# Layer 0 attention: scores on 32x64 pieces of the array, reciprocals of row sums on transposed blocks, five groups of key tiles added up

## The chip, the core and the metric

The kernel runs on one core of one Trainium2 chip. A core has five engines that work side by side and wait for each other by semaphores: TensorE (PE in the profile; its weight loads are a row of their own, PEld), VectorE (DVE), ScalarE (ACT), GpSimd (POOL) and SyncE (SP), which here issues DMAs. The metric is the device time of one execution, in microseconds (us). Matmuls write to PSUM, which here is used as six banks for three score tiles and two banks for two accumulators; everything else lies in SBUF.

## The reference

Four layers, each of the form x = x + f(groupnorm(x)), on x of 2 images, 128 channels, 64x64 pixels. Only layer 0 is touched by the change. Its f, cut to what matters:

```python
xn = biasfree_ln(x, ln1_w)
qkv = conv1x1(xn, w_qkv)
qkv = depthwise_conv3x3(qkv, w_dw)
q1, k1, v, q2, k2 = split(qkv, 5)                 # 4 heads of 32 channels, 4096 tokens
q1, q2, k1, k2 = l2norm over the tokens
attn1 = softmax(einsum('bhnc,bhmc->bhnm', q1, k1) * temperature)   # 4096 x 4096 per head
out1 = einsum('bhnm,bhmc->bhnc', attn1, v)
attn2 = softmax(einsum('bhnc,bhnd->bhcd', q2, k2) * temperature)   # 32 x 32 per head
out2 = einsum('bhnc,bhcd->bhnd', v, attn2)
out = conv1x1(out1 + out2, w_po)
out = conv1x1(biasfree_ln(out, ln2_w), w_proj) + b_proj
```

Layer 1 is a sum of small convolutions and correlations, layer 2 a quaternion convolution by FFT, layer 3 a softmax attention with 8 heads over the same 4096 tokens.

## The kernel before, in words

All is float32. For each image, layer 0 first runs its convolutions, then the large attention (`attention`, line 1750), then `finish` (line 1803), which multiplies by the output weights and is woven into the convolutions of the next image.

The attention goes over 8 blocks of 512 queries (`qb`), and in each over 32 tiles of 128 keys (`kt`); a pair of the two is a step here. One step of `_attn_four` (line 1333) does this for all four heads:

- four score matmuls (line 1341), one per head `j`. The stationary operand is 32 channels by 128 keys of `k1`, the moving one 32 channels by 512 queries of `q1`. Head `j` lies in partitions 32j to 32j+31, so that the four use four different row groups of the array. The result, keys by queries, goes to a PSUM tile of two heads (`ps_s`, two tiles a step out of three buffers).
- two exps on ScalarE (line 1350), one for each PSUM tile, into a `weights` tile of 128 x 4 x 512 in SBUF (four buffers).
- for the step before, `multiply` (line 1774): four value matmuls (line 1757), each 128 keys by 32 channels of `vt`, which write 32 partitions each of one accumulator, `ac[0]`. They use four column groups of the array and add up over the 32 key tiles of the block.

The softmax needs the sums over the keys as well. VectorE adds up the weights of `SUMMED` = 8 key tiles into one `sums` tile (line 1792, seven additions a group, since the first tile of a group is only remembered), and `sums` (line 1759) multiplies each finished group by a matrix of ones of 32 columns into the second accumulator, `ac[1]`: four matmuls, again of line 1757, for each of four groups in a block. It is called at the fourth step of the group after. As ones have 32 equal columns, each row sum comes out 32 times, once for each channel of its head.

With the last group of a block, `sums` also divides: ScalarE copies the accumulator (line 1770) into a tile with the tag `g`, which has one buffer and is used for the normalised input of the next image as well (line 1484); VectorE takes reciprocals of its 128 x 512 elements (line 1771) and multiplies the values by them into `q1` (line 1772), whose queries of this block are no longer needed. The values have been copied to `used` by ScalarE at the last key tile (line 1782).

Other work is woven in: every four steps of the attention one piece of a side list goes in (`_weave`). The list is the small channel attention of both images, and for image 0 the normalisation of image 1 (`normalize`, line 1473), for image 1 some statistics.

Within the convolutions and `finish` the order of each engine's instructions is that of the program. Within the attention it isn't held: there the planner of the tile framework orders the instructions by the program's order and by its own estimate of when they are ready. Each engine then works through its own queue in that order, and waits where an operand isn't there.

Of the kernel before, what the change touches and what calls it, by code (L numbers as in the profile page):

```python
# [10 lines left out]
F32 = mybir.dt.float32  # L11
# [7 lines left out]
CH = 512  # L19
NCH = S // CH  # L20
ROWS = CH // W
NQT = S // 128
# [92 lines left out]
def _weave(main, side, every):  # L115

    for n, _ in enumerate(main):
        if n % every == every - 1:
            next(side, None)
    for _ in side:  # L120
        pass
# [1163 lines left out]


LIMIT = 60.0
SUMMED = 8
F32R = mybir.dt.float32r
ENGINES = (  # L1290
    mybir.EngineType.PE,
# [41 lines left out]
def _attn_four(nc, p_pool, ps_pool, q, k, multiply):  # L1333

    waiting = []
    for qb in range(NCH):
        for kt in range(NQT):
            ps = [ps_pool.tile([128, 2, CH], F32, tag="sp", name="ps_s") for _ in range(2)]
            for j in range(4):
                rows = slice(32 * j, 32 * j + 32)  # L1340
                nc.tensor.matmul(  # L1341
                    ps[j // 2][:, j % 2, :],
                    k[rows, kt * 128 : (kt + 1) * 128],
                    q[rows, qb * CH : (qb + 1) * CH],
                    start=True,
                    stop=True,
                )
            w = p_pool.tile([128, 4, CH], F32, tag="weights", name="weights")
            for p in range(2):
                nc.scalar.activation(w[:, 2 * p : 2 * p + 2, :], ps[p], AF.Exp)  # L1350
            waiting.append((qb, kt, w))
            if len(waiting) > 1:
                multiply(*waiting.pop(0))
            yield
    for x in waiting:
        multiply(*x)
    yield
# [49 lines left out]
def _layer0(ctx, tc, X, a, cst, worst, there, dram):  # L1407
    nc = tc.nc
    one = ctx.enter_context(tc.tile_pool(name="f0_one", bufs=1))
    small = ctx.enter_context(tc.tile_pool(name="f0_small", bufs=2))  # L1410
    cp = ctx.enter_context(tc.tile_pool(name="f0_ch", bufs=2))
# [6 lines left out]
    def acc(n):  # L1418
        return accp.tile([128, CH], F32, tag=f"acc{n}", name=f"ps_acc{n}")
# [14 lines left out]
    q1 = one.tile([128, S], F32, name="q1")  # L1434
# [7 lines left out]
    ones = one.tile([128, 32], F32, name="ones")  # L1442
# [307 lines left out]
    def attention(pool, side):  # L1750
        ac = [None, None]
        parts, pending, used = [None], [], {}

        def four(n, lhs, w, first, last):
            for j in range(4):
                rows = slice(32 * j, 32 * j + 32)
                nc.tensor.matmul(ac[n][rows, :], lhs(rows), w[:, j, :], start=first, stop=last)  # L1757

        def sums():

            while pending:
                qb, n, w = pending.pop(0)
                if n == 0:
                    ac[1] = acc(1)
                four(1, lambda rows: ones, w, n == 0, n == NQT // SUMMED - 1)
                if n == NQT // SUMMED - 1:

                    cols = slice(qb * CH, (qb + 1) * CH)
                    rec = cp.tile([128, CH], F32, tag="g", name="rec", bufs=1)
                    nc.scalar.copy(rec, ac[1])  # L1770
                    nc.vector.reciprocal(rec, rec)
                    nc.vector.tensor_mul(q1[:, cols], used.pop(qb), rec)

        def multiply(qb, kt, w):


            if kt == 0:
                ac[0] = acc(0)
            four(0, lambda rows: vt[:, kt, rows], w, kt == 0, kt == NQT - 1)
            if kt == NQT - 1:  # L1780
                used[qb] = pool.tile([128, CH], F32, tag="used", name="used", bufs=2)
                nc.scalar.copy(used[qb], ac[0])  # L1782
            i = kt % SUMMED
            if i == 3:
                sums()
            if i == 0:
                parts[0] = w
            else:
                t = parts[0]
                if i == 1:  # L1790
                    parts[0] = pool.tile([128, 4, CH], F32, tag="sums", name="sums", bufs=2)
                nc.vector.tensor_add(  # L1792
                    parts[0].rearrange("p j c -> p (j c)"),
                    t.rearrange("p j c -> p (j c)"),
                    w.rearrange("p j c -> p (j c)"),
                )
            if i == SUMMED - 1:
                pending.append((qb, kt // SUMMED, parts[0]))

        _weave(_attn_four(nc, pool, spp, q1, k1, multiply), side, 4)  # L1800
        sums()

    def finish(b, w2):
# [78 lines left out]
    for b in range(B):  # L1882
        w2 = small.tile([128, 128], F32, tag="w2", name="w2")
        with tc.tile_pool(name="f0_conv", bufs=1) as pool, _in_order(tc):
            ss2, own = convolutions(pool, b, before)
        if b == 0:

            with _after(tc):
                rows_of_weights = _weights_by_rows(nc, dram, a)
        side = [channel_attention(ss2, own, w2)]  # L1890
        if b + 1 < B:
            side.append(normalize(b + 1))
        if b:
            side.append(
                _stats_steps(
                    nc,
                    small,
                    lambda: sp()[:, 0, :],
                    X[:, b - 1, :],
                    cst,  # L1900
                    mhalf,
                    there[:, b - 1],
                )
            )
        with tc.tile_pool(name="f0_p", bufs=4) as pool:
            attention(pool, chain(*side))
        before = finish(b, w2)
# [434 lines left out]
```

## Time and profile before

| what | time |
|---|---|
| median of three runs | 4225.66 us (4211.73 to 4226.44) |
| span of the profiled execution, which has no other time of its own | 4221.3 us |
| attention of image 0 | about 191 to 815 us of the span |
| attention of image 1 | about 1016 to 1609 us |
| one block of 512 queries, undisturbed | 72.71 us |
| blocks 0, 1, 2 of image 0 | 83.9, 93.3, 75.7 us |
| blocks 0 and 2 of image 1 | 77.8, 75.6 us |
| busy in an undisturbed block (665.5 to 738.2 us) | PE 72.4, DVE 67.6, ACT 63.0 us |
| busy over the whole span | PE 4050.3, DVE 2186.7, ACT 3342.7 us |

How to read it: "busy" of TensorE is not its bound, because its records overlap[...]. The time of one of TensorE's stages is read from the start of one group to the start of the next. Each float32 matmul leaves two records of a load and two of a matmul, called its first and second pass below. Idle time is given with what ended it.

### The profile page before, as it was taken

To read this page: it belongs to the slowest core of one execution; us is meant where nothing else is said; L and a number is where in the kernel's file an instruction comes from. 1 tells how busy PE (TensorE), PEld (TensorE's weight loads), DVE (VectorE), ACT (ScalarE), POOL (GpSimd) and SP (SyncE) were. 2 spreads that over 40 slices of the span, in tenths; PEclk is the share of its full clock that TensorE was granted. 3 is DMA by queue.
4 is the path that set the end of the run, shared out by engine and by line. 5 is a ranking of instruction groups with operands and counts; after the bars stand their busy time and mean duration, and the time that the engine had idled before them with its cause. 6 is when DMAs were issued, how large, how long until landed. Compare 5 with 4: busy or idle time off the path is not lost. (4 is left out here: it accounts for less than half of the span.)

```text
span 4221.3 us, 82246 instructions
## 1 busy us (share of the span) xinstructions
PE 4050.3 (96%) x35790; PEld 1548.6 (37%) x35790; DVE 2186.7 (52%) x2358; ACT 3342.7 (79%) x4051; POOL 71.6 (2%) x145
## 2 busy tenths in 40 slices
PE   7999999989999998997999999999999999999998
PEld 4523222354222224445664333333333333333332
DVE  4679999757899998986765212221032102211111
ACT  4478888735888883326646999999999999999998
POOL 1001000010000001000000000000000000000000
PEclk9999999999999998998999999999999999999999
DMA  1299950000000000004650000000000000000000
GB/s 48 28 194 191 186 64 1 1 2 2 1 1 1 1 1 12 1 1 170 273 222 4 6 6 4 6 6 6 4 6 6 4 6 6 6 4 6 6 6 5
DMA packets 158822, 158.86 MB, mean 38 GB/s; under 512 B 24809, under 2 KB 148713, under 8 KB 154354
## 3 DMA queue, kind: packets, MB, share of 16 engines
q1 hardware_dynamic: 158450, 153.50, 15.6%
q8 instruction: 282, 4.62, 0.4%
q14 instruction: 90, 0.74, 0.1%
HBM read 145.09 MB, written 73.40 MB: 52 GB/s over the span
## 5 line engine op out<-in xcount | busy, mean ns | idle before, releaser
L2104 ACT ACTIVATE weights<-ps_s 128x1024 f32<-128x1024 f32 x2048 | 1885.2, 1104 | 65.9 <-PE ps_s L2094 65.4
L1350 ACT ACTIVATE weights<-ps_s 128x1024 f32<-128x1024 f32 x1024 | 992.8, 1022 | 178.6 <-PE ps_s L1341 154.0
L2113 PE MATMUL ps_acc<-weights,vt 128*32 128x512 f32 x8192 | 1095.5, 607 | 0.0
L2094 PE MATMUL ps_s<-q,k 32*128 32x512 f32 x8192 | 925.8, 445 | 5.2 <-ACT weights L2104 5.2
L1792 DVE TENSOR_TENSOR sums<-sums,weights 128x2048 f32<-128x2048 f32 x384 | 879.2, 2289 | 43.1 <-ACT weights L1350 8.2
L2094 PEld LDWEIGHTS ps_s<-q,k 32*128 32x128 f32 x8192 | 472.7, 183 | 842.0 <-ACT weights L2104 775.2
L1341 PE MATMUL ps_s<-q,k 32*128 32x512 f32 x4096 | 649.3, 643 | 3.7 <-ACT weights L1350 1.3
L2135 DVE COPY u<-ps_acc 128x512 f32<-128x512 f32 x32 | 22.1, 692 | 1041.3 <-PE ps_acc L2113 1041.3
L1757 PE MATMUL ps_acc<-weights,vt 128*32 128x512 f32 x4096 | 550.4, 607 | 3.4 <-ACT used L1782 3.2
L1341 PEld LDWEIGHTS ps_s<-q,k 32*128 32x128 f32 x4096 | 210.5, 184 | 431.4 <-issue 212.9
L2113 PEld LDWEIGHTS ps_acc<-weights,vt 128*32 128x32 f32 x8192 | 163.1, 108 | 378.4 <-issue 366.5
L1757 PEld LDWEIGHTS ps_acc<-weights,vt 128*32 128x32 f32 x4096 | 81.1, 108 | 396.6 <-issue 378.4
L662 DVE SCALAR_TENSOR_TENSOR X<-g,w,X 128x2048 f32<-128x2048 f32 x84 | 197.4, 2351 | 2.6
L1792 DVE TENSOR_TENSOR sums<-weights 128x2048 f32<-128x2048 f32 x64 | 146.5, 2290 | 65.2 <-ACT weights L1350 65.2
L1546 PE MATMUL ps_sp<-pad,diag 32*32 32x512 f32 x4608 | 159.7, 599 | 2.3 <-ACT q L1566 1.3
L1008 PE MATMUL ps_z<-w_ri,e 128*32 128x128 f32 x2048 | 137.4, 409 | 14.6 <-DVE e L950 12.2
L2055 DVE TENSOR_TENSOR vt<-ps_acc,bv 128x384 f32<-128x384 f32 x32 | 17.8, 557 | 247.0 <-PE ps_acc L2048 247.0
L2025 DVE LOAD_MASK_SELECT qq<-ps_acc x32 | 0.4, 14 | 222.5 <-PE ps_acc L2022 222.5
L1546 PEld LDWEIGHTS ps_sp<-pad,diag 32*32 32x32 f32 x4608 | 95.0, 103 | 55.6 <-issue 17.7
L2138 DVE RECIPROCAL r<-r 128x512 f32<-128x512 f32 x32 | 107.3, 3354 | 1.1
L950 DVE TENSOR_SCALAR e<-ps_pe 32x136 f32<-32x136 f32 (+1 forms) x352 | 104.4, 297 | 4.9
L948 ACT ACTIVATE e<-ps_pe 32x136 f32<-32x136 f32 (+1 forms) x352 | 99.4, 282 | 4.1
(288 smaller groups left out, 2586.4 us busy)
## 6 DMA issues: line engine op xcount, KB each, us to landing
w_ri<-w_r SPq DMA_DIRECT2D x16, 2112.0 KB, 8.1
w_ri<-w_i SPq DMA_DIRECT2D x16, 2112.0 KB, 13.7
w_r<-in_L_conv_kr_w SPq DMA_DIRECT2D x15, 528.0 KB, 12.7
w_r<-in_L_conv_kr_x SPq DMA_DIRECT2D x15, 528.0 KB, 12.5
w_r<-in_L_conv_kr_y SPq DMA_DIRECT2D x15, 528.0 KB, 12.3
w_r<-in_L_conv_kr_z SPq DMA_DIRECT2D x15, 528.0 KB, 12.6
w_i<-in_L_conv_ki_w SPq DMA_DIRECT2D x15, 528.0 KB, 12.6
w_i<-in_L_conv_ki_x SPq DMA_DIRECT2D x15, 528.0 KB, 12.5
```

What stands on the lines that cost most here:

```text
L662: nc.vector.scalar_tensor_tensor(xi, g[:, i : i + H // 2, j : j + W], w8[:, s : s + 1], xi, ALU.mult, ALU.add)
L950: nc.vector.tensor_scalar_mul(out, got[of, :, s], sign)
L1008: nc.tensor.matmul(out.rearrange("p (n f o) -> p n f o", n=2, f=2), e[:, s, 2 * j : 2 * j + 2, :].rearrange("p f x -> p (f x)"), w.rearran ...
L1341: nc.tensor.matmul(ps[j // 2][:, j % 2, :], k[rows, kt * 128 : (kt + 1) * 128], q[rows, qb * CH : (qb + 1) * CH], start=True, stop=True,)
L1350: nc.scalar.activation(w[:, 2 * p : 2 * p + 2, :], ps[p], AF.Exp)
L1546: nc.tensor.matmul(ps[r // 2][to, r % 2, :].rearrange("p (h w) -> p h w", w=W), diag[rows, grp, t, :], pad[rows, y0 : y0 + ROWS, t % 3 : t ...
L1757: nc.tensor.matmul(ac[n][rows, :], lhs(rows), w[:, j, :], start=first, stop=last)
L1792: nc.vector.tensor_add(parts[0].rearrange("p j c -> p (j c)"), t.rearrange("p j c -> p (j c)"), w.rearrange("p j c -> p (j c)"),)
L2094: nc.tensor.matmul(ps[j // 2][:, j % 2, :], k[rows, kt * 128 : (kt + 1) * 128], q[n][rows, qb * CH : (qb + 1) * CH], start=(n == 0), stop= ...
L2104: nc.scalar.activation(w[p], ps[p], AF.Exp)
L2113: nc.tensor.matmul(ac[0][32 * j : 32 * j + 32, :], vt[:, kt, j // 2, i : i + 2, :].rearrange("p a d -> p (a d)"), w[j // 2][:, i, :], star ...
L2138: nc.vector.reciprocal(r, r)
```

## The change

Three edits, all in layer 0's attention.

- Each score matmul is split in two by keys: 64 keys of one head to the lower 64 partitions of the PSUM tile, 64 to the upper. There are eight matmuls in a step, on eight pieces of 32 rows and 64 columns of the array.
- A block's 32 key tiles form five groups, of 7, 6, 7, 6 and 6, in place of four groups of 8. VectorE makes 27 additions in a block, TensorE five sets of four matmuls with ones. The set of a group still comes at the fourth step of the group after.
- The copy and the reciprocal over 512 columns go. VectorE transposes the accumulator in blocks of 32x32 straight from PSUM; since the 32 rows of a head are equal, each transposed block has 32 equal columns, and the first column of each of the 16 blocks holds all 512 sums. The reciprocal runs over these 128 x 16 elements, a second transpose spreads them over 32 columns by a repeated read and brings them back into `q1`, and the product follows in place. Only the transposed sums are in the buffer with the tag `g`.

```diff
-SUMMED = 8
+SUMMED = (7, 6, 7, 6, 6)
...
-                nc.tensor.matmul(
-                    ps[j // 2][:, j % 2, :],
-                    k[rows, kt * 128 : (kt + 1) * 128],
-                    q[rows, qb * CH : (qb + 1) * CH],
-                    start=True,
-                    stop=True,
-                )
+                for half in range(2):
+                    to = slice(64 * half, 64 * half + 64)
+                    nc.tensor.matmul(
+                        ps[j // 2][to, j % 2, :],
+                        k[rows, kt * 128 + 64 * half : kt * 128 + 64 * half + 64],
+                        q[rows, qb * CH : (qb + 1) * CH],
+                        start=True,
+                        stop=True,
+                    )
...
+        places = [(n, i) for n, size in enumerate(SUMMED) for i in range(size)]
...
-                four(1, lambda rows: ones, w, n == 0, n == NQT // SUMMED - 1)
-                if n == NQT // SUMMED - 1:
+                four(1, lambda rows: ones, w, n == 0, n == len(SUMMED) - 1)
+                if n == len(SUMMED) - 1:
 
                     cols = slice(qb * CH, (qb + 1) * CH)
-                    rec = cp.tile([128, CH], F32, tag="g", name="rec", bufs=1)
-                    nc.scalar.copy(rec, ac[1])
-                    nc.vector.reciprocal(rec, rec)
-                    nc.vector.tensor_mul(q1[:, cols], used.pop(qb), rec)
+                    by_query = cp.tile([128, CH // 32, 32], F32, tag="g", name="by_query", bufs=1)
+                    nc.vector.transpose(by_query.rearrange("p n i -> p (n i)"), ac[1])
+                    rec = small.tile([128, CH // 32], F32, tag="rec", name="rec")
+                    nc.vector.reciprocal(rec, by_query[:, :, 0])
+                    nc.vector.transpose(
+                        q1[:, cols].rearrange("p (n i) -> p n i", i=32),
+                        rec.unsqueeze(2).to_broadcast([128, CH // 32, 32]),
+                    )
+                    nc.vector.tensor_mul(q1[:, cols], used.pop(qb), q1[:, cols])
...
-            i = kt % SUMMED
+            n, i = places[kt]
...
-            if i == SUMMED - 1:
-                pending.append((qb, kt // SUMMED, parts[0]))
+            if i == SUMMED[n] - 1:
+                pending.append((qb, n, parts[0]))
```

## The prediction

> **What bounds the kernel now.** I read the page, then the lines of the attention of layer 0, then single instructions in time order in an undisturbed block of 512 queries. The columns of a group are: line, engine, operation, tiles, shape, count, busy us, mean ns, idle before it and its releaser.
>
> ```profile
> span 4221.3 us, 82246 instructions
> ...
> L1350 ACT ACTIVATE weights<-ps_s 128x1024 f32<-128x1024 f32 x1024 | 992.8, 1022 | 178.6 <-PE ps_s L1341 154.0
> L1341 PE MATMUL ps_s<-q,k 32*128 32x512 f32 x4096 | 649.3, 643 | 3.7 <-ACT weights L1350 1.3 <-DVE st L1371 1.0 <-DVE n L1718 0.8
> L1341 PEld LDWEIGHTS ps_s<-q,k 32*128 32x128 f32 x4096 | 210.5, 184 | 431.4 <-issue 212.9 <-PE ps_s L1341 183.6 <-ACT weights L1350 23.2
> L1757 PE MATMUL ps_acc<-sums,ones 128*32 128x512 f32 x512 | 67.7, 593 | 1.8 <-DVE sums L1792 1.8
> L1771 DVE RECIPROCAL rec<-rec 128x512 f32<-128x512 f32 x16 | 53.5, 3346 | 1.8 <-ACT rec L1770 1.8
> L1017 DVE STREAM_TRANSPOSE z<-ps_z 128x512 f32<-128x512 f32 x64 | 45.1, 712 | 24.7 <-PE ps_z L1008 23.6
> L1546 PEld LDWEIGHTS ps_sp<-pad,diag 32*32 32x32 f32 x4608 | 95.0, 103 | 55.6 <-issue 17.7 <-DVE vt L1557 2.5 <-DVE y L1470 0.6
> ```
>
> ScalarE waits for TensorE's scores (154 us); each float32 matmul is two records, so 2048 score matmuls stand as 4096. The timeline of TensorE has the cycle:
>
> ```profile
> 700.79 1.31 PE L1341 MATMUL ps_s<-q,k 32*128 32x512 f32 x8
> 702.04 1.06 PE L1757 MATMUL ps_acc<-weights,vt 128*32 128x512 f32 x8
> 703.03 1.14 PE L1341 MATMUL ps_s<-q,k 32*128 32x512 f32 x8
> 704.10 1.06 PE L1757 MATMUL ps_acc<-weights,vt 128*32 128x512 f32 x8
> 705.10 1.31 PE L1341 MATMUL ps_s<-q,k 32*128 32x512 f32 x8
> ```
>
> Score stages alternate, 1.24 us to the next stage and 1.07; value stages take 0.996. Two steps are 4.304 us. In the long one the third matmul starts 0.185 late: its PSUM buffer is freed by the first exp of the step before. So the path is: scores, first exp, second half of the next scores, values. The start of one exp follows that of the other by 0.92 us, so ScalarE needs 3.69 of 4.304 and isn't the bound. VectorE is close: per block 28 additions at 2.396 start to start are 67.1, and reciprocal and product with gaps 4.2: 71.3 of 72.71 us per undisturbed block (11 of 16).
>
> Two places are different. In block 1 of image 0 (this view is VectorE, then ScalarE, then TensorE):
>
> ```profile
> 297.65 3.35 DVE L1771 RECIPROCAL rec<-rec 128x512 f32<-128x512 f32 x1
> 300.92 2.23 DVE L1792 TENSOR_TENSOR sums<-sums,weights 128x2048 f32<-128x2048 f32 x1
> 303.06 0.68 DVE L1772 TENSOR_TENSOR q<-used,rec 128x512 f32<-128x512 f32 x1
> ...
> 303.78 0.81 ACT L1484 ACTIVATE g<-X,gn_shift,gn_got 128x512 f32<-128x512 f32 x1 [5.51 <-DVE q L1772]
> ...
> 304.64 1.11 PE L1495 MATMUL ps_sp<-consts,g 128*128 128x128 f32 x4 [5.06 <-ACT g L1484]
> ```
>
> The normalisation's g shares one buffer with rec, and ScalarE stands 5.51 us until the product has read rec; TensorE then idles 5.06. And after the last block of each image nothing covers the reciprocal:
>
> ```profile
> 814.91 0.59 ACT L1770 COPY rec<-ps_acc 128x512 f32<-128x512 f32 x1 [2.34 <-PE ps_acc L1757]
> ...
> 819.76 1.93 ACT L1531 COPY pad<-ps_sp 128x1024 f32<-128x1024 f32 x2 [4.27 <-DVE q L1772]
> ```
>
> **What the skill says.** "TensorE: Matmul & The Clock Gate", section "LDWEIGHTS (loading the stationary operand)", prices a load by its columns at 1.2 per ns, whatever the rows. The trace agrees: 32x32 loads take 0.101 us, 32x128 ones 0.181, which is 0.83 ns a column. "TensorEngine Tiling (Array Packing)", section "Tiling Modes", allows eight 32x64 tiles and says that a change of mode drains the array. The trace has this as a load that isn't covered at the start of each stage: second passes start 0.453 after the first behind a load of 0.106 (values), 0.533 behind 0.181 (scores), so 0.352 plus the load. The first page's "Part 3: Packing small matmuls" gives some 4 ns per further tile; here starts are 6.6 ns apart, with 4 tiles and in the 32x32 convolutions with the first 8. "VectorE: DVE Perf Modes", section "The three transpose paths", has the vector transpose work on 32x32 blocks; L1017 prices one at 0.712.
>
> **The change part by part.**
>
> *Scores.* Four matmuls become eight, with 64 columns each. No trace row has a 32x64 load; between 0.101 and 0.181 the slope gives 0.101 + 32 x 0.00083 = 0.128, which I take. Bounds: below 0.101 (no cheaper than 32 columns), above 0.181, or 0.256 if the two halves of one row group load one after the other. Now the cycle, from the start of a short score stage. Before: second pass of the first half's last matmul at 0.540, exp 0.634 later (1.174), buffer free 1.077 later (2.251), second half's last second pass 0.540 later (2.791), values 0.518 later (3.309), next scores 0.996 later: 4.305, measured 4.304. After: last second pass of a half at 0.352 + 0.128 + 3 x 0.0066 = 0.500; exp 1.134; free 2.211; 2.711; 3.229; 4.225. Gain 0.079 per pair, 16 pairs per block, 16 blocks: -20.2 us. TensorE alone would need 2 x (0.996 + 1.045) = 4.08, ScalarE 3.69: neither takes over.
>
> *Groups of 7, 6, 7, 6, 6.* A fifth set of four matmuls with ones per block. Its price is in the single instructions: values to sums 0.883 and sums to scores 0.972, in place of 0.996: 0.859. It runs on TensorE, the path, with no cover. Since groups of 7 put it behind a short score stage, one delayed half per block (0.15) falls into it: 0.71 x 16 = +11.4; bounds 8.9 (two fall in) and 13.7 (none). VectorE does 27 additions, not 28: 2.4 per block. In undisturbed blocks that hides behind TensorE, worth nothing. In the blocks 0 of both images VectorE has other work beside it, and TensorE's sums wait for it (up to 2.7 us at a time in the first); there I take -2 in all; bounds 0 and -5.
>
> *Reciprocals.* Gone: the ScalarE copy (0.586) and a reciprocal over 512 columns (3.346). New on VectorE: a transpose out of PSUM (0.712), a reciprocal over 16 (a 128x1 one takes 0.158, slope 0.0062 per column: 0.25), a transpose back from a broadcast (not in the trace; 0.69 like the 128x512 vector operations, bounds 0.6 and 1.3), the product (0.68). With gaps 2.6 in place of 4.2. VectorE then has 27 x 2.396 + 2.6 = 67.3 of about 72 us, so all this is covered in undisturbed blocks, and the copy gone frees ScalarE, not the path: -1, bounds 0 and -2. The first transpose now waits for TensorE itself; behind it in VectorE's queue stand additions, and behind those, four steps later, the exps that reuse their weights buffers (four of them). If it stood a whole addition too early, some 2 us of stall would be within the 4.7 us of slack; without that cover it would cost 2 x 16 = 32 us.
> At the two image ends, 0.62 + 3.45 + 0.69 = 4.8 us become 2.6: -4.4, bounds -3 and -5. At the g buffer, only the first transpose and the short reciprocal hold it, about 1 us in place of 6.1: -5, and TensorE's following stage at 1.87 in place of 1.0, slowed after its idling, may go too: I take -6, bounds 0 and -8. What is late next there is TensorE's own work.
>
> Sum: -20.2 + 11.4 - 2 - 1 - 4.4 - 6 = -22.2. Against the span of 4221.3 that is 4199; the runs' median lies 4.4 above that span, so 4203. No DMA is added or moved.
>
> **Rivals.** (A, forecast) as summed; own range 4188 to 4219, the bounds of the small terms. (B) The delayed half vanishes: if the first halves finish enough earlier, the pair falls to TensorE's own 4.08: a further 0.145 x 256 = -37, 4166. For it: the delay is small, and a first half that ends 0.15 sooner than I have it is enough. Against: all eight tiles stream at once, so that nothing lets the first half end early, and the exp of 1.08 us still lies between. (C) The smaller pieces buy nothing: the load shows as 0.181, pair 4.331, +7 + 11.4 - 13.4 = +5: 4231. For it: no 64-column load is in the trace. (D) Slower: the two loads of a row group follow each other, at the start of every score stage, 0.256 visible. The pair is 4.304 + 0.177, +45 + 11.4 - 13.4 = +43: 4269. It decides for slower from a visible load of 0.213 on, since each 0.01 costs 0.02 per pair, 5 us. Against it: in the 32x32 convolutions four column tiles of one row group load 7 ns apart.
>
> **Chances.** A 0.56, B 0.14, C 0.13, D 0.17. A run-to-run difference of 0.5% (21 us) is about what can be told from no change; A straddles that bound: 0.33 faster, 0.23 same. So faster 0.33 + 0.14 = 0.47, same 0.23 + 0.13 = 0.36, slower 0.17. The range, 4165 to 4248, takes in A and C, B but for its tail, and D up to a visible load of 0.215.
>
> **What would show it.** Right: score loads of about 0.128, second passes 0.48 after the first, pairs of 4.22, 640 records at sums with ones in place of 512 (and 8192 score matmuls), no L1770 copy, g waiting under 1.5 us in block 1, blocks near 72.1 us. Wrong: 64-column loads above 0.15; VectorE idle ahead of its first transpose with exps waiting for VectorE in every block; score stages longer than 1.24; or an order of the planner in which sums with ones or additions stand elsewhere than at the fourth step of a group.

## The result, and the profile after

Over 20 runs each, the kernel before has a median of 4219.6 us (4207.9 to 4229.7) and the changed one 4209.3 us (4197.7 to 4211.8). The ratio is 0.9971, with a 95% interval of 0.9964 to 0.9977: 10 to 15 us less, inside the 0.5% that was set as the bound for a difference. 4203 was forecast; the direction is right, and about half of the 22 us came.

The profiled executions differ by more: spans of 4221.3 and 4195.9 us. That of the changed kernel is its fastest run (4197.72 us), and the stretch behind the last exp of layer 0, where only the last division of image 1 differs, is 2616.7 us in the one and 2606.0 in the other. So the spans aren't compared below, but the parts.

The page of the changed kernel has these lines in place of those of before (the last is the first tile of each group's addition):

```profile
span 4195.9 us, 90633 instructions
...
L1352 ACT ACTIVATE weights<-ps_s 128x1024 f32<-128x1024 f32 x1024 | 992.9, 1023 | 180.6 <-PE ps_s L1343 164.2
L1343 PE MATMUL ps_s<-q,k 32*64 32x512 f32 x8192 | 627.3, 613 | 7.1 <-ACT weights L1352 2.4
L1343 PEld LDWEIGHTS ps_s<-q,k 32*64 32x64 f32 x8192 | 159.6, 130 | 436.4 <-PE ps_s L1343 320.3
L1760 PE MATMUL ps_acc<-sums,ones 128*32 128x512 f32 x640 | 84.4, 592 | 1.3 <-DVE sums L1800 1.3
L1800 DVE TENSOR_TENSOR sums<-weights 128x2048 f32<-128x2048 f32 x80 | 183.3, 2291 | 113.6 <-ACT weights L1352 113.6
```

The load of 64 columns takes 0.130 us; the forecast had 0.128. The matmuls with ones have 640 records in place of 512, and they stood idle for VectorE 1.3 us in all (1.8 before). ScalarE still waits for scores (164 us in place of 154). The timeline of TensorE in a block without other work:

```profile
662.28 1.11 PE L1343 MATMUL ps_s<-q,k 32*64 32x512 f32 x16
663.33 1.06 PE L1760 MATMUL ps_acc<-weights,vt 128*32 128x512 f32 x8
664.32 1.28 PE L1343 MATMUL ps_s<-q,k 32*64 32x512 f32 x16
665.53 1.06 PE L1760 MATMUL ps_acc<-weights,vt 128*32 128x512 f32 x8
666.53 1.12 PE L1343 MATMUL ps_s<-q,k 32*64 32x512 f32 x16
```

A score stage takes 1.05 or 1.21 us to the start of the next stage, a value stage 0.99 or 1.00, a pair of steps 4.245 us by the unrounded starts (4.304 before). In the long stage the second half still starts late, 0.191 us after the stage's first piece where a short stage has 0.027: the chain through the first exp is as it was.

Block 1 of image 0, VectorE and then ScalarE:

```profile
291.84 0.71 DVE L1773 STREAM_TRANSPOSE by_query<-ps_acc 128x512 f32<-128x512 f32 x1
292.48 2.25 DVE L1800 TENSOR_TENSOR sums<-sums,weights 128x2048 f32<-128x2048 f32 x1
294.65 0.24 DVE L1775 RECIPROCAL rec<-by_query 128x16 f32<-128x16 f32 x1
294.92 0.71 DVE L1776 STREAM_TRANSPOSE q<-rec 128x512 f32<-128x512 f32 x1
295.67 0.69 DVE L1780 TENSOR_TENSOR q<-used,q 128x512 f32<-128x512 f32 x1
...
294.92 0.81 ACT L1486 ACTIVATE g<-X,gn_shift,gn_got 128x512 f32<-128x512 f32 x1 [3.61 <-DVE rec L1775]
```

The normalisation's g waits 3.61 us, where it waited 5.51. The short reciprocal is the last reader of the shared buffer, and the planner has put a whole addition between it and the transpose ahead of it.

At the end of image 0 (ScalarE) the copies for the next convolution begin 3.30 us after the last second pass of the matmuls with ones, in place of 5.51; the product at the end of image 1 ends 3.26 us after it, in place of 5.53:

```profile
810.49 1.93 ACT L1533 COPY pad<-ps_sp 128x1024 f32<-128x1024 f32 x2 [4.98 <-DVE q L1780]
```

Start to start of the first exp of a block, us, with two profiles of each kernel (the second ones are the last experiment):

| part | before | before, second profile | after | after, second profile |
|---|---|---|---|---|
| undisturbed block | 72.71 | 72.71 | 72.49 | 72.49 |
| image 0, blocks 0 and 1 together | 177.23 | 175.06 | 172.82 | 172.91 |
| image 0, block 2 | 75.68 | 75.68 | 75.07 | 75.08 |
| last exp of image 0 to first of image 1 | 206.34 | 203.97 | 199.93 | 199.99 |
| image 1, block 0 | 77.75 | 77.75 | 78.97 | 78.97 |
| image 1, block 2 | 75.58 | 75.58 | 74.35 | 74.35 |
| all of this, first exp of image 0 to last of image 1 | 1410.10 | 1405.52 | 1396.43 | 1396.60 |
| from there to the end | 2616.7 | 2611.8 | 2606.0 | 2616.2 |

With about 2.2 us more at the end of image 1, the two attentions and what lies between them are 11 to 16 us shorter; the ratio says 10 to 15.

### The profile page after: what moved, and what is told of

It is laid out like the page before. It is cut to its first block, busy times and chain, and to the rows that moved or that the text cites. A ratio compares the mean times of both kernels' runs of the same rounds, so it can differ in the third digit from the quotient of the medians.

```text
span 4195.9 us, 90633 instructions
## 1 busy us (share of the span) xinstructions
PE 4026.9 (96%) x40014; PEld 1494.0 (36%) x40014; DVE 2127.8 (51%) x2374; ACT 3332.9 (79%) x4035; POOL 71.3 (2%) x145
## 3 DMA queue, kind: packets, MB, share of 16 engines
HBM read 145.09 MB, written 73.40 MB: 52 GB/s over the span
## 5 line engine op out<-in xcount | busy, mean ns | idle before, releaser
L2102 PE MATMUL ps_s<-q,k 32*128 32x512 f32 x8192 | 924.9, 444 | 5.4 <-ACT weights L2112 5.4
L1800 DVE TENSOR_TENSOR sums<-sums,weights 128x2048 f32<-128x2048 f32 x352 | 806.7, 2292 | 38.4 <-ACT weights L1352 5.2
L2102 PEld LDWEIGHTS ps_s<-q,k 32*128 32x128 f32 x8192 | 471.2, 182 | 839.4 <-ACT weights L2112 773.6
L1343 PE MATMUL ps_s<-q,k 32*64 32x512 f32 x8192 | 627.3, 613 | 7.1 <-ACT weights L1352 2.4
L1343 PEld LDWEIGHTS ps_s<-q,k 32*64 32x64 f32 x8192 | 159.6, 130 | 436.4 <-PE ps_s L1343 320.3
L1800 DVE TENSOR_TENSOR sums<-weights 128x2048 f32<-128x2048 f32 x80 | 183.3, 2291 | 113.6 <-ACT weights L1352 113.6
```

Source lines behind the costliest of these rows:

```text
L1343: nc.tensor.matmul(ps[j // 2][to, j % 2, :], k[rows, kt * 128 + 64 * half : kt * 128 + 64 * half + 64], q[rows, qb * CH : (qb + 1) * CH], ...
L1800: nc.vector.tensor_add(parts[0].rearrange("p j c -> p (j c)"), t.rearrange("p j c -> p (j c)"), w.rearrange("p j c -> p (j c)"),)
L2102: nc.tensor.matmul(ps[j // 2][:, j % 2, :], k[rows, kt * 128 : (kt + 1) * 128], q[n][rows, qb * CH : (qb + 1) * CH], start=(n == 0), stop= ...
```

## The experiments

The theory is that of the forecast: the scores gain, the fifth set of matmuls with ones is a cost, and the reciprocals gain at the ends and at g. The rival for the scores and the groups is VectorE: that it bounds a block near 72.2 us, so that the scores alone gain little and the groups pay by its relief. All kernels compute the whole reference. Half-rate time, below, is time in which the trace shows one half as the granted clock of TensorE.

**Scores alone.** The kernel before with the new score matmuls only.

```diff
-                    ps[j // 2][:, j % 2, :],
-                    k[rows, kt * 128 : (kt + 1) * 128],
...
+                for half in range(2):
+                    to = slice(64 * half, 64 * half + 64)
...
+                        ps[j // 2][to, j % 2, :],
+                        k[rows, kt * 128 + 64 * half : kt * 128 + 64 * half + 64],
```

> The kernel before with the score matmuls on 32x64 pieces alone. Chain theory (scores, first exp, second half of the next scores, values set the time): a pair of steps takes 4.245 us as in the changed kernel in place of 4.304, an undisturbed block 71.75 us in place of 72.71, the whole 15 us less than before (ratio 0.9964). VectorE theory (VectorE, with 71.3 us of work a block, takes over as soon as scores get shorter): blocks of 72.2 us or more with exps waiting for VectorE, ratio 0.998 or above.

Measured: ratio 0.9974 (0.9965 to 0.9982), 4209.5 us; undisturbed blocks 71.80 us, 0.91 less than before. VectorE isn't the bound: by the forecast's sum it works 71.3 of 71.8 us of a block, and with the shorter reciprocals as well the block is no shorter (71.79, the fourth run below). By the block the scores are worth 16 x 0.91 = 14.6 us, where 20.2 had been summed; the interval of the ratio says 8 to 15.

**Groups alone.** The kernel before with groups of 7, 6, 7, 6, 6.

```diff
-SUMMED = 8
+SUMMED = (7, 6, 7, 6, 6)
```

> The kernel before with groups of 7, 6, 7, 6, 6 alone. Chain theory: the fifth set of matmuls with ones costs 0.74 us a block, undisturbed blocks of 73.45 us, the whole 12 us more than before (ratio 1.0028). VectorE theory (one addition less is worth 2.4 us in each block in which VectorE is late): the blocks 0 to 2 of both images get 2 us shorter, and the whole is at most 4 us longer.

Measured: 1.0022 (1.0013 to 1.0032), 4227.5 us; undisturbed blocks 73.40 us, 0.69 more than before. In the blocks 0, where the relief of VectorE was to show, it takes 85.01 and 79.56 us in place of 83.92 and 77.75. On balance the relief gains nothing there either, and the theory of a gain through VectorE falls. The fourth run shows what the blocks 0 lose.

**Reciprocals alone.**

```diff
-                    rec = cp.tile([128, CH], F32, tag="g", name="rec", bufs=1)
-                    nc.scalar.copy(rec, ac[1])
-                    nc.vector.reciprocal(rec, rec)
-                    nc.vector.tensor_mul(q1[:, cols], used.pop(qb), rec)
+                    by_query = cp.tile([128, CH // 32, 32], F32, tag="g", name="by_query", bufs=1)
+                    nc.vector.transpose(by_query.rearrange("p n i -> p (n i)"), ac[1])
...
```

> The kernel before with the reciprocals on transposed blocks alone. Chain theory: undisturbed blocks stay at 72.6 to 72.7 us; block 1 of image 0 loses about 4.7 us and each end of an attention 2.2 us; the whole 10 us less (ratio 0.9976). Rival (the reciprocal matters in every block, since VectorE is nearly full): 1 us or more per block, 20 us or more in all (0.995).

Measured: 0.9981 (0.9975 to 0.9987), 4211.4 us. Undisturbed blocks 72.71 us, as before; block 2 of image 1 74.54 in place of 75.58; both ends 2.2 us shorter. Block 1 of image 0 takes 90.34 us, where 4.7 less than 93.31 had been expected. With the same half-rate time, 10.2 us, the second profile of before has 91.46, so that 1.1 us is left for the edit. The wait at g (timeline of ScalarE) is shorter by 2 us, not by 4.5:

```profile
296.70 0.81 ACT L1484 ACTIVATE g<-X,gn_shift,gn_got 128x512 f32<-128x512 f32 x1 [3.52 <-DVE rec L1772]
```

**Scores and reciprocals, four groups of 8.** The changed kernel without its groups.

```diff
-SUMMED = (7, 6, 7, 6, 6)
+SUMMED = 8
```

> The changed kernel with four groups of 8 again: scores on 32x64 pieces and the new reciprocals, nothing else. Chain theory: undisturbed blocks of 71.75 us, 0.74 less than the changed kernel; the whole 12 us less than the changed kernel, about 0.9943 of before. VectorE theory (28 additions at 2.396 and 2.6 for the reciprocals are 69.7 us, and they come late at the wrong places): exps wait for VectorE, blocks of 72.5 us or more, no faster than the changed kernel (0.997).

Measured: 0.9948 (0.9930 to 0.9965), 4197.7 us. Undisturbed blocks 71.79 us, so that the fifth set costs 72.49 - 71.79 = 0.70 us a block here too, 11.2 us in all. VectorE around g has the same order as in the changed kernel, so the addition that stands in the way doesn't come from the groups:

```profile
291.43 0.71 DVE L1772 STREAM_TRANSPOSE by_query<-ps_acc 128x512 f32<-128x512 f32 x1
292.06 2.25 DVE L1799 TENSOR_TENSOR sums<-sums,weights 128x2048 f32<-128x2048 f32 x1
294.23 0.24 DVE L1774 RECIPROCAL rec<-by_query 128x16 f32<-128x16 f32 x1
```

The blocks 0 take 83.07 and 77.12 us here, 84.44 and 78.97 in the changed kernel. There TensorE stops before a score stage for a copy of other work (line 1743, `a2t`). The copy empties one of the PSUM tiles that scores use too, and it stands behind additions in VectorE's queue. With four groups of 8, a set with ones happens to stand in that pause and costs nothing (TensorE, this kernel):

```profile
243.72 1.04 PE L1759 MATMUL ps_acc<-sums,ones 128*32 128x512 f32 x8
245.02 1.12 PE L1343 MATMUL ps_s<-q,k 32*64 32x512 f32 x16 [0.25 <-DVE a2t L1743]
```

With five groups no set stands there, and TensorE is idle (the changed kernel):

```profile
242.58 1.06 PE L1760 MATMUL ps_acc<-weights,vt 128*32 128x512 f32 x8
244.81 1.12 PE L1343 MATMUL ps_s<-q,k 32*64 32x512 f32 x16 [1.16 <-DVE a2t L1743]
```

The same happens some 20 us later at the copy of line 1748 (0.45 us idle in the changed kernel, no wait over 0.15 here). The two pauses grow by 0.9 and 0.3 us in each image. The longest wait for sums, in block 0 of image 0, falls from 1.8 to 1.3 us. With the fifth set of 0.70 these make 1.4 and 1.9 us; the blocks 0 differ by 1.37 and 1.85.

**The same, without the shared buffer.** The first transpose writes into `q1`.

```diff
-                    by_query = cp.tile([128, CH // 32, 32], F32, tag="g", name="by_query", bufs=1)
-                    nc.vector.transpose(by_query.rearrange("p n i -> p (n i)"), ac[1])
+                    by_query = q1[:, cols].rearrange("p (n i) -> p n i", i=32)
+                    nc.vector.transpose(q1[:, cols], ac[1])
```

> The kernel of the fourth run (scores and reciprocals, four groups), with the first transpose written into q1 itself, so that nothing of the division is in the buffer g. Chain theory: in block 1 of image 0 ScalarE no longer waits 3.6 us for the short reciprocal, TensorE no longer slows down after it; that block goes from 86.87 to about 83 us and the rest stays; the whole 3 to 4 us less than the fourth run, 0.994 of before. Rival (g is late anyway, the wait only moves): block 1 stays above 86 us.

Measured: 0.9931 (0.9918 to 0.9943), 4190.0 us. Block 1 of image 0 takes 82.03 us in place of 86.87, and the clock isn't at half rate anywhere in it (3.4 us of half rate in the fourth run). The undisturbed blocks are 71.79 again; the stretch between the attentions is 201.47 in place of 200.37 us. The medians are 7.7 us apart, but the two intervals overlap.

**Sixteen pieces of 32x32.** The kernel with scores and reciprocals, with pieces of half the width.

```diff
-                for half in range(2):
-                    to = slice(64 * half, 64 * half + 64)
+                for part in range(4):
+                    to = slice(32 * part, 32 * part + 32)
```

> The kernel of the fourth run with sixteen score matmuls of 32x32 in place of eight of 32x64: the load is 0.101 us in place of 0.130, but four more matmuls lie ahead of the end of each half. If the exp comes 0.01 us later for each further piece of a half (the reading of the 0.020 us by which my cycle missed), pairs take about 4.28 us, undisturbed blocks 72.4, the whole 10 us more than the fourth run. If the 0.020 us is a fixed delay of column tiles, pairs stay at 4.245, blocks at 71.8 and the whole at the fourth run's time.

Measured: 0.9968 (0.9958 to 0.9977), 4207.9 us; pairs of about 4.288 us and blocks mostly of 72.55. The load is shorter, and the kernel is slower:

```profile
L1343 PEld LDWEIGHTS ps_s<-q,k 32*32 32x32 f32 x16384 | 156.6, 103 | 439.1 <-PE ps_s L1343 335.4 <-issue 61.5 <-ACT weights L1352 21.3
```

What grows is the time from the last second pass of a half to its exp: 0.634 us with two pieces in a half (before), 0.654 with four, 0.694 with eight. That is 0.010 us for each further piece.

**Order of the pieces turned.** In each PSUM tile first the lower halves of both heads, then the upper ones, so that neighbours in the order use different row groups.

```diff
-            for j in range(4):
-                for half in range(2):
+            for p in range(2):
+                for half in range(2):
+                    for j in (2 * p, 2 * p + 1):
```

> The kernel of the fourth run with the order of the score matmuls turned: in each half first the lower 64 keys of both heads, then the upper 64, so that two pieces of one row group are not issued one after the other. If neighbours in a row group hold each other up, the 0.020 us goes: pairs 4.225, blocks 71.5, the whole 5 us less than the fourth run. If it comes from the number of pieces, nothing changes: blocks 71.8.

Measured: 0.9951 (0.9934 to 0.9968), 4199.3 us, and 71.79 us for undisturbed blocks: no difference to the order before. The 0.020 us that the exp is later doesn't come from two neighbours in a row group; it goes with the number of pieces. The number of column groups (1, 2 and 4) grows along with the pieces in these kernels, so they can't tell the two apart. A hint: where ScalarE's copies of line 1770 waited in the kernel before, for four pieces in four column groups, they start 0.649 to 0.660 us after the last second pass, which is near the 0.654 of four pieces and not the 0.694 of four column groups; but those pieces have 128 rows.

**Only the buffer.** The kernel before, with the long reciprocals in `q1` in place of the shared buffer.

```diff
-                    rec = cp.tile([128, CH], F32, tag="g", name="rec", bufs=1)
+                    rec = q1[:, cols]
```

> The kernel before with rec in q1 itself, so that the long reciprocal no longer holds the buffer g; nothing else. If the wait for g is a cost of its own, as the prediction's -6 has it, block 1 of image 0 gets 5 to 8 us shorter (93.3 to 85 to 88) and the whole about 5 us; undisturbed blocks stay at 72.7 and the ends of the attentions as they were. Rival: what block 1 lost in the changed kernel was the clock of TensorE in that one execution, and the wait only moves: block 1 at 91 us or more in the profile, no difference in the times.

Measured: 0.9996 (0.9988 to 1.0004), 4220.8 us: no difference. The wait is gone: blocks 0 and 1 take 169.27 us together, where the two profiles of before have 177.23 and 175.06. Part of it comes back at once, since the exps now wait for VectorE in the stretch behind the reciprocal (timeline of ScalarE):

```profile
302.17 1.94 ACT L1350 ACTIVATE weights<-ps_s 128x1024 f32<-128x1024 f32 x2 [0.27 <-PE ps_s L1341]
304.69 1.94 ACT L1350 ACTIVATE weights<-ps_s 128x1024 f32<-128x1024 f32 x2 [0.58 <-DVE sums L1792]
```

That is already in the 169.27. The stretch from the last exp of image 0 to the first of image 1 took 208.13 us (206.34 and 203.97 before). So of 6 to 8 us, 2 to 4 went again in this execution; why none is left in the median isn't shown.

**Three groups.** The changed kernel with groups of 11, 11 and 10: 29 additions a block, three sets of matmuls with ones.

```diff
-SUMMED = (7, 6, 7, 6, 6)
+SUMMED = (11, 11, 10)
```

> The changed kernel with three groups, of 11, 11 and 10, in place of five. Chain theory alone: two sets of matmuls with ones less than the changed kernel, undisturbed blocks of 71.0 us, the whole 24 us less. VectorE theory: 29 additions at 2.396 and 2.6 for the division are 72.1 us, VectorE is late for good and exps wait for their weights buffers, blocks of 72.1 us or more. I expect VectorE to be the bound here, and only here.

Measured: 0.9944 (0.9928 to 0.9961), 4195.5 us. Undisturbed blocks take 70.71 us at first and 71.06 to 71.38 later, less than expected. VectorE becomes the bound only here, and only just. From these groups of ScalarE and VectorE one reads that exps wait for additions 2.5 us in all, where the changed kernel's row names no such wait:

```profile
L1352 ACT ACTIVATE weights<-ps_s 128x1024 f32<-128x1024 f32 x1024 | 993.1, 1023 | 160.4 <-PE ps_s L1343 140.9 <-DVE sums L1800 2.5
L1800 DVE TENSOR_TENSOR sums<-sums,weights 128x2048 f32<-128x2048 f32 x416 | 953.2, 2291 | 47.1 <-ACT weights L1352 7.1 <-DVE sums L1800 0.5 <-DVE st L1373 0.4
```

In the timeline of VectorE nine additions in a row, from 686.69 to 708.06 us, are 2.374 apart, and the four new operations take 2.39: 29 x 2.374 + 2.39 = 71.2, where the expectation had come to 72.1. The blocks 0 are long, 85.64 and 79.59 us, and at the ends of the images the last group comes later: 6.81 us from the last exp of image 0 to the last second pass with ones, in place of 4.45. In the blocks 0, TensorE stops 2.00 us for the copy of line 1743, where the changed kernel stops 1.16; both blocks also have 3.4 us of half-rate time here, and none there.

**Three groups, without the shared buffer.** The three groups, and the first transpose into `q1`, together.

> The kernel of the fifth run (nothing in g) with three groups, of 11, 11 and 10. Undisturbed blocks of 70.7 to 71.4 us in place of 71.8, but 2.2 us more at each end and 2 to 3 us more in each block 0, where VectorE is late. I expect 4188, 2 us less than the fifth run; if VectorE is the bound after all, no less than it.

Measured: 0.9927 (0.9913 to 0.9942), 4194.3 us; blocks 70.71 to 71.11 us, block 1 of image 0 83.08. It can't be told from the kernel with four groups and no shared buffer (0.9931); both beat the kernel before and the changed one.

The shared buffer has now been given up in three pairs of kernels. In the profiles of all three, block 1 gets shorter (by 3.6 to 7.7 us) and the stretch between the attentions longer: 208.13 against 206.34 and 203.97 us, 201.47 against 200.37, 207.93 against 203.53, with 3.4 to 10.2 us more of half-rate time in it. So a part of what block 1 gains was lost again in that stretch. With one or two executions of a kernel, it isn't shown that it must be.

**The kernel before, a second profile.**

> The kernel before once more, unchanged, for a second profile. What block 1 of image 0 lost (93.31 us before, 88.38 after the change) is either a cost of that block's order, which comes again each time, or partly half-rate time of TensorE's clock in one execution (17.1 us of it stood in block 1). Theory of the clock: the wait of g is again 5.5 us, blocks without other work are again 72.71, but the half-rate time in block 1 is another and the block's length moves with it by about half of the difference; with 6.8 us of half-rate time it would be about 88 to 90. Theory of the order: 93.3 again, within 0.5 us, whatever the clock does.

Measured: 4214.3 us. The half-rate time is 10.2 us in block 1, not 15.0 (a further 2.1 of what the expectation counted lay in the end of block 0), and the block takes 91.46 us, not 93.31; g waits 5.68 us; undisturbed blocks are 72.71. This agrees with the theory of the clock: 1.85 us for 4.8 us of half rate. It doesn't explain it all: at the same rate the 6.8 us of half rate that the changed kernel has would leave 91.46 - 3.4 x 0.39 = 90.1 us, and that has 88.4.

**The changed kernel, a second profile.**

> The changed kernel once more, unchanged, for a second profile; its first was of an execution of 4197.7 us, the fastest, with a mean clock of 0.985. Theory of the clock: an execution near the median (4209) has a mean clock near 0.982 and a span longer by about 2.6 us for each 0.001 of clock, with undisturbed blocks again at 72.49 and all of the difference in the block 1s, blocks 2 and the convolutions between the attentions, where TensorE idles. Rival: undisturbed blocks differ too, above 72.6.

Measured: 4208.8 us, near the median. Every stretch from the first exp to the end of the attentions is within about 0.1 us of the first profile's, block 1 and the convolutions too; 10.2 of the 11 us lie in the rest, 2606.04 and 2616.25 us, with 97.9 and 125.1 us of it at half rate. The theory of the clock had put it into the attentions' idle places; it is in other layers. The view by stretches gives the stretch and its length, then the busy time and count of PE, PEld, DVE, ACT and POOL, the granted clock (PEclk), the DMA share and GB/s. From the last exp of image 0 to the first of image 1, before:

```profile
809.81:1016.15 206.34, 178.79 (x2771) 109.34 (x2768) 112.53 (x172) 76.94 (x133) 13.49 (x40) 0.95 0.01 2
```

the kernel before in its second profile:

```profile
808.27:1012.24 203.97, 175.41 (x2771) 108.11 (x2768) 112.53 (x172) 76.94 (x132) 13.50 (x40) 0.97 0.01 2
```

and the changed kernel, this stretch and the rest of the program, in its second profile:

```profile
803.45:1003.44 199.99, 173.49 (x2777) 106.96 (x2780) 110.49 (x174) 76.31 (x131) 13.46 (x40) 0.97 0.01 2
1590.66:4206.91 2616.25, 2523.95 (x21639) 1031.93 (x21639) 875.65 (x1405) 2159.74 (x2697) 22.17 (x40) 0.98 0.09 32
```

The same kernel before takes 2.4 us less for the same work where the clock is higher. The changed kernel's 4.0 us against the second profile are 2.2 of the shorter end, and 1.8 that stand beside 10.2 us of half rate in place of 13.7. At what the two profiles of before lost here, 2.4 us for 6.8 us of half rate, 3.4 us would be some 1.2 (an estimate); the rest is open.

## Why the prediction was right or wrong

| term of the sum | predicted | measured |
|---|---|---|
| 256 pairs of steps, scores | -20.2 | -15.1 (4.304 to 4.245 us) |
| fifth set of matmuls with ones, 16 blocks | +11.4 | +11.2 (0.70 a block) |
| relief of VectorE in blocks 0 | -2 | about +1.8 (-0.5 from a shorter wait for sums, +2.4 from longer waits for copies) |
| reciprocals in undisturbed blocks | -1 | 0 |
| two image ends | -4.4 | -4.5 |
| g in block 1 | -6 | about -1 to -3 |

The measured column sums to about -8 to -10 us, with another 1 us in block 2 of image 1, where the reciprocals alone gave as much. The ratio, 10 to 15 us, has the clock in it too: over the 20 runs of the changed kernel a line of time against mean granted clock falls by 2.6 us for 0.001 (42 runs of before: 2.7), and at 0.981 the two lines are 8.5 us apart.

That 4209 lies near the 4203 of the forecast is in part luck. The forecast set out from the median of three runs of before, 4225.7 us, which 20 runs put at 4219.6; from there its 22.2 us lead to 4197.4, which is 12 us below what was measured. Its own range, 4188 to 4219, reaches up to no change at all (4219.6), so that the evidence for the mechanism is in the traces and not in the median. A gain beyond 0.5% had been held likelier than none (0.47 to 0.36) and did not come.

*Scores.* Right in its mechanism: the load is 0.130 us, second passes start 0.480 after the first, pieces 6.6 ns apart, the buffer is free 1.077 after the exp starts, and the delayed half stays. The Trainium skill's page "TensorE: Matmul & The Clock Gate", section "LDWEIGHTS (loading the stationary operand)", makes the time of a load its columns at 1.2 per ns. The trace agrees in the slope alone: 32, 64 and 128 columns take 0.101, 0.130 and 0.181 us, some 0.075 us more than columns divided by 1.2 each, and it was the prediction's slope between two measured loads that carried the price. The term was mis-sized in the step "exp 0.634 later": it is 0.654, and 0.020 for each pair is 5.1 us. The kernel with sixteen pieces shows that this time grows with the pieces of a half. Undisturbed blocks are 72.49 us for that, not the 72.1 named as a sign. Rivals B, C and D, which hung on the delayed half and on the load, are refuted by the same numbers: the load isn't 0.181 or 0.256, and the delayed half is still there.

*Groups.* Right to 0.02 us a block; the two kernels that take the groups away or add them alone agree. The failed part is VectorE's relief in the blocks 0, "there I take -2 in all". The 2.7 us that the prediction read as the longest wait for sums is that of the loads; the matmuls with ones themselves stood 1.8 us for VectorE in all before, and the relief took 0.5 of it. These blocks got longer, by 1.37 and 1.85 us against the kernel with the other two edits, of which 0.70 is the set itself. The rest is that TensorE waits longer for two copies of VectorE, since with five groups no set with ones falls into these pauses. The prediction had given where the sets stand no price but that of a delayed half.

*Reciprocals.* The ends were right to 0.1 us. The g term failed in "only the first transpose and the short reciprocal hold it, about 1 us": the prediction took them as neighbours, and the planner put 2.25 us of addition between. Its own lines of before had shown the like: an addition, at 300.92 us, between the reciprocal and the product. The wait fell by 1.9 us only, to 3.61, where under 1.5 had been named. Even the wait's full price is in doubt: to take it away in the kernel before gave nothing in the median (-5 to +2 us by the interval), while in the kernels with short reciprocals it took 0.0017 off the ratio twice, each time within the intervals. At equal half-rate time, the reciprocals alone shorten block 1 by 1.1 us. So -6 isn't supported, and what g is worth in the changed kernel stays open.

*The split of the change.* The scores gain, and the groups give most of it back: with the fifth set undone the ratio is 0.9948 in place of 0.9971. Their intervals (0.9930 to 0.9965, 0.9964 to 0.9977) touch, but the 0.70 us in every block is beyond doubt. The prediction's own numbers said as much, 71.3 us of VectorE work hidden in a block of 72.7.

## What to carry to other kernels

A smaller stationary operand shortens a stage where its load isn't covered, here 0.83 ns a column; but each further piece costs its own time at the end, here 0.010 us, so that eight pieces of 64 columns beat both four of 128 and sixteen of 32. Before an engine is relieved at another's cost, ask in a profile whether anything waits for it: extra sets of matmuls on the path were paid in full for a relief of which 0.5 us was used. Look as well at which work stands in pauses: a set with ones cost nothing while TensorE had to wait for a copy anyway, and the new groups moved it out of there. Where a buffer's hold is to get shorter, check what the order written by a planner puts between its first and its last user.

## What the runs showed that was not expected

- A wait for a PSUM tile that several matmuls fill ends later the more there are, from the same last start: 0.634, 0.654 and 0.694 us with two, four and eight. That the pieces cost at their end, and not in their 6.6 ns from start to start alone, had not been in the sum.
- The Trainium skill's "TensorE: Matmul & The Clock Gate", "Part 1: The HAM clock gate", has TensorE's clock at half its rate after an idle window of about 3.4 us. The traces agree with the length: the stretches at half rate last 3.4, 6.8, 10.2 or 17.1 us, but for one that the end of the program cuts. Their sum was 166.4 and 135.6 us in the two profiles of the kernel before. Blocks without other work never have one in these four profiles; block 1 of image 0 (once from the end of block 0 on), the convolutions between the attentions and the other layers do. Where two profiles of one kernel differ in a stretch, 0.24 to 0.39 us went with each us at half rate. Their spans were 9 and 11 us apart, most of it in such stretches. That is as much as the whole change is worth, which is why single spans can't judge it.
